# Layer 1 attention: softmax sums of two row blocks inverted in one instruction, the split of the probabilities two steps behind, attention output and projection one step later

## The chip, the cores and the metric

The kernel runs on one core of one Trainium2 chip, in one launch, and holds a whole two-layer model. The metric is the device time of one execution in microseconds. The engines that matter here are TensorE (PE in the profile; its weight loads are PEld), VectorE (DVE), ScalarE (ACT), GpSimd (POOL) and SyncE (SP), which issues most of the DMAs.

## The reference, cut to what matters

The input is `x` with 2 batches of 1024 rows of 512 numbers. Layer 0 is an attention with one head of 128 and a branch with a Sinkhorn iteration. Layer 1, which takes most of the time, is a causal attention with 32 query heads of 128, whose keys and values come in 8 groups (four query heads share one), and beside it a feed-forward part with a low-rank mixture of experts.

```python
xn = _layernorm(x)
x = x + _L1_attn_ref(xn, ...) + _L1_ffn_ref(xn, ...)

def _L1_attn_ref(hidden_states, Wq, Wk_down, Wv_down, Wk_up, Wv_up, Wo):
    q = ...                                       # 32 heads of 128
    k, v = ...                                    # 8 groups of 128, repeated 4 times
    scores = jnp.einsum('bhqd,bhkd->bhqk', q, k) * scale
    scores = jnp.where(causal, scores, -1e9)
    attn = jax.nn.softmax(scores, axis=-1)
    out = jnp.einsum('bhqk,bhkd->bhqd', attn, v)
    return out.transpose(0, 2, 1, 3).reshape(b, s, H * D) @ Wo.T
```

The change touches only how the softmax of layer 1 is divided by its sums, and when.

## The kernel before, in words

Every product of two float32 matrices is done with float16 pairs: each operand is kept as a high part and a low part (what the high part leaves over), and three matmuls (high by high, high by low, low by high) make one product. `mm3` (line 89) issues them for projections and scores, `attn_out` (line 365) for the product of probabilities and values.

Layer 1 runs over 16 groups `g`: eight key/value groups of batch 0 and then eight of batch 1. A group has 32 steps `s`. One step handles one row block: 32 query positions of four heads, which fill the 128 partitions, against the first W = 32(s+1) keys. What one row block goes through:

- scores on PE (`rows_scores`, line 89) into one PSUM bank of tag `s` up to W = 512, else into two; there are four such banks (`BS`)
- row maximum on DVE (`rows_exp`, lines 284 and 288), which also writes the scaled scores from PSUM into the SBUF tile `P`
- exponential on ACT (line 292), in place in `P`, which also adds up the row into the small tile `r`
- `rows_hi`: reciprocal of the sum on DVE (line 316), a scaling of it by 16384 on ACT (line 317), and the high part of the probabilities on ACT (line 322) into the tile `Phl`
- `rows_lo`: the low part on DVE (line 330; two instructions for some widths), a memset of padding on POOL (line 334), and a transposing DMA from `Phl` to the tile `PT` on SP's queue (line 335)

`row_step` interleaves two row blocks: in step s it emits the scores of block s, then `rows_hi` of block s-1, then the row maximum and exponential of block s, then `rows_lo` of block s-1. A list called `pending` holds the one block in between. `P` and `Phl` have three buffers each (`PB`, `LB`). A buffer of `P` holds four blocks for s below 8, two for s below 16, and one from there on. So from s = 16 the row maximum of block s+3 can only write once the low part of block s has been computed.

After each `row_step` come the other pieces of work that a table `fill` assigns to the step: query projections, keys and values of the next group, fetching and splitting weights (POOL, held behind the latest `rows_lo` by `behind`), and the work of the other parts of the model (`extra`). For each of the 16 pairs of row blocks the product with the values runs at step 4c + 2k + `AVD` (`av`; c counts blocks of four steps, k the pair in it), and for each c the output projection at step 4c + `WOD` (`wo`). A pair's `av` comes three steps after the step that emits the second transpose of the pair.

This text order is not the order on the engines. When the program is built, the framework's scheduler goes through a simulated time and gives each engine, whenever it is free, the earliest-written instruction that is ready. The order on each engine is then fixed, and on the chip each engine works through its list in order and waits at the head of it for the semaphores of the instruction there.

Layer 0 uses the same `row_step` with blocks of 128 rows.

Of the kernel before, what the change touches and what calls it, by code (L numbers as in the profile page):

```python
# [11 lines left out]
AF = mybir.ActivationFunctionType  # L12
# [4 lines left out]
P = 128  # L17
# [12 lines left out]
QR = 32  # L30
# [9 lines left out]
SK0, SKN, MX0, MXN, LN1 = 1, 116, 122, 74, 198  # L40

G0, G1, GL, WT, LX, LA = 16, 200, 3, 220, 231, 240
AVD, WOD = 5, 10
KVN, QN, QNN, QH = 19, 18, 24, 1
MG = range(8, 16)
FW, FF = 210, 221
# [2 lines left out]
PSCALE = 16384.0  # L49
# [3 lines left out]
def tile_model(ctx: ExitStack, tc: tile.TileContext, out: bass.AP, a: dict):  # L53
# [3 lines left out]
    V, A, G = nc.vector, nc.scalar, nc.gpsimd  # L57
# [7 lines left out]
    def T(tag, shape, dt=F32, bufs=None):  # L65
        count[0] += 1
        kw = {} if bufs is None else {"bufs": bufs}
        return sb.tile(shape, dt, tag=tag, name=f"{tag}_{count[0]}", **kw)
# [115 lines left out]
    last_hi, last_lo, last_low = [None], [None], [None]  # L184
# [87 lines left out]

    P_of, hl_of = [None], [None]

    def rows_exp(pieces, causal, scale, n, k):

        W = pieces[-1][0] + pieces[-1][1]
        Pm = share(P_of, n, k, lambda: T("P", [P, n, S // n], bufs=PB))
        nm = T("nm", [P, 2], bufs=4)
        last = None  # L280
        for k, (o, w, pt) in enumerate(pieces):
            first = 1.0e30 if last is None else last
            if causal and o + w == W:
                last_row[0] = V.tensor_tensor_reduce(Pm[:, o:o + w], pt[:, :w], mask[:, 512 - w:],  # L284
                                       -scale, first, ALU.add, ALU.min,
                                       nm[:, k:k + 1])
            else:
                last_row[0] = V.tensor_scalar(Pm[:, o:o + w], pt[:, :w], -scale, first,  # L288
                                ALU.mult, ALU.min, accum_out=nm[:, k:k + 1])
            last = nm[:, k:k + 1]  # L290
        r = T("r", [P, 2], bufs=4)
        A.activation(Pm[:, :W], Pm[:, :W], AF.Exp, bias=last, scale=-1.0,  # L292
                     accum_out=r[:, 0:1])
        return Pm, r, W

    def rows_parts(W, n, k, mix=False):

# [14 lines left out]
        v = hl.rearrange("p (l k) -> p l k", l=2)  # L312
        return hl, v[:, 0, :W], [(0, W, v[:, 1, :W])], v[:, :, W:] if W < m * P else None

    def rows_hi(Pm, r, W, pool, hl):
        V.reciprocal(r[:, 1:2], r[:, 0:1])  # L316
        A.activation(r[:, 1:2], r[:, 1:2], AF.Copy, scale=PSCALE)  # L317
        if pool:
            A.activation(Pm[:, :W], Pm[:, :W], AF.Copy, scale=r[:, 1:2])
            A.activation(hl[1], Pm[:, :W], AF.Copy)  # L320
        else:
            A.activation(hl[1], Pm[:, :W], AF.Copy, scale=r[:, 1:2])  # L322

    def rows_lo(Pm, r, W, pool, hl, dst):
        whole, hi, los, pad = hl
        for a0, a1, lo in los:
            if pool:
                G.tensor_tensor(lo, Pm[:, a0:a1], hi[:, a0:a1], ALU.subtract)
            else:
                last_low[0] = V.scalar_tensor_tensor(lo, Pm[:, a0:a1], r[:, 1:2], hi[:, a0:a1],  # L330
                                                     ALU.mult, ALU.subtract)
        if pad is not None:

            behind(G.memset(pad, 0.0), last_low[0])  # L334
        nc.sync.dma_start_transpose(dst[:, :whole.shape[1] // P], whole)  # L335

    pending = []

    def row_step(q=None, K=None, W=None, causal=None, scale=None, dst=None, pool=None, n=1, k=0,
                 mix=False):  # L340

        if q is not None:
            pieces = rows_scores(q, K, W)
        old = None
        if pending:
            old = pending.pop()
            rows_hi(*old[:5])
        if q is not None:
            pending.append((*rows_exp(pieces, causal, scale, n, k), pool, rows_parts(W, n, k, mix), dst))
        if old:  # L350
            rows_lo(*old)

    def out_tile():
        count[0] += 1
# [311 lines left out]
    SC1 = 1.0 / (math.sqrt(128.0) * 128.0)  # L666
# [108 lines left out]
    def fetch_q(g, hh):  # L775
        qw[g, hh] = fetch(a["Wq"][4 * (g % NG) + hh])
# [8 lines left out]
    def layer1_attn(kv0, start, extra):  # L785


        N, NS = NB * NG, S // QR
        fill = {}

        def at(g, s, f):
            g, s = g + s // NS, s % NS
            fill.setdefault((g, s), []).append(f)

        kvs, Qs, PTs, avs, aos, wos = [{} for _ in range(6)]

        def twice(g):
            Vm = kvs[g]["Vm"] = [T("xr", [P, NT, P], F16, bufs=XB) for l in range(2)]
            for l in range(2):
                for k in range(2):  # L800
                    nc.sync.dma_start(Vm[l][64 * k:64 * k + 64], kvs[g]["V"][0:64, l])

        def q_unit(g, u):
            half, hh = divmod(u, 4)
            if hh == 0:
                Qs[g, half] = T("Q", [P, 2, NS // 2, 4, QR], F16, bufs=2)
            qproj(g // NG, qw[g, hh], Qs[g, half], hh, half)

        def fetch_wo(g, hh):
            n = 4 * (g % NG) + hh  # L810
            wos[g, hh] = fetch(a["WoT"][n * P:(n + 1) * P, :])

        def split_wo(g, hh):
            wos[g, hh] = parts_of(wos[g, hh], "wo", 32.0, WB)

        def av(g, c, k):
            if k == 0:
                avs[g, c] = out_tile()
            aos[g, c] = group_av(kvs[g]["V"], kvs[g].get("Vm"), PTs[g, 2 * c + k], c, k, avs[g, c])

        def wo(g, c):
            wo_block(g // NG, c, aos[g, c], [wos[g, h] for h in range(4)], g % NG == NG - 1)

        kvs[0], fs = kv0
        start(fs[2:], lambda u: q_unit(0, u))
        for hh in range(4):
            fetch_wo(0, hh)
            split_wo(0, hh)
        for g in range(N):
            if g + 1 < N:  # L830
                new = (g + 1) % NG == 0
                kvs[g + 1], fs = kv((g + 1) // NG, (g + 1) % NG)
                at(g, KVN - 2 if new else 1, fs[0])
                for k, f in enumerate(fs[1:]):
                    at(g, KVN + 2 * k if new else 1 + 4 * k + 2 * (k == 0), f)
                for hh in range(4):
                    at(g, 5 + 4 * hh, lambda g=g, hh=hh: fetch_q(g + 1, hh))
                    at(g, 7 + 4 * hh, lambda g=g, hh=hh: split_q(g + 1, hh))
                for u in range(4):
                    at(g, QNN + 2 * u if new else QN + 4 * u, lambda g=g, u=u: q_unit(g + 1, u))  # L840
                for hh in range(4):
                    s = 26 + 2 * hh if new else 22 + 3 * hh
                    at(g, s - 2, lambda g=g, hh=hh: fetch_wo(g + 1, hh))
                    at(g, s, lambda g=g, hh=hh: split_wo(g + 1, hh))
            for u in range(4):
                at(g, QH + (1 if (g + 1) % NG == 0 else 3) * u, lambda g=g, u=u: q_unit(g, 4 + u))
            if g in MG:
                at(g, 2, lambda g=g: twice(g))
            for c in range(NT):
                for k in range(2):  # L850
                    at(g, 4 * c + 2 * k + AVD, lambda g=g, c=c, k=k: av(g, c, k))
                at(g, 4 * c + WOD, lambda g=g, c=c: wo(g, c))
        for k, fs in extra.items():
            fill[k] = fs + fill.get(k, [])
        for g in range(N + 1):
            for s in range(NS):
                if g < N:
                    c, r = divmod(s, NR)

                    n = 4 if c < 2 else 2 if c < 4 else 1  # L860
                    if c < 4 and r == 0:
                        PT = T("PT", [P, 2 * (c + 1), NR, P], F16, bufs=3)
                        for k in range(2):
                            PTs[g, 2 * c + k] = PT[:, :, 2 * k:2 * k + 2]
                    elif c >= 4 and r % 2 == 0:
                        PTs[g, s // 2] = T("PT", [P, 2 * (c + 1), 2, P], F16, bufs=3)
                    Qt, q0 = Qs[g, s // (NS // 2)], s % (NS // 2)
                    row_step(lambda l: Qt[:, l, q0].rearrange("p h q -> p (h q)"),
                             kvs[g]["K"], QR * (s + 1), True, SC1, PTs[g, s // 2][:, :, r % 2], False, n, r, g in MG)
                elif pending:  # L870
                    row_step()
                for f in fill.pop((g, s), []):
                    f()
        assert not fill, sorted(fill)
# [131 lines left out]
    PTs = attn0_rows(0, 0, *f0[0][:2], lambda: adv(CA))  # L1006
    ys0 = branch0(0, *f0[0][3:5], lambda: adv(CB))
    attn0_out(0, 0, f0[0][2], PTs)
    PTs = attn0_rows(0, 1, *f0[0][:2], lambda: adv(CA))
# [6 lines left out]
    for half in range(2):  # L1016
# [5 lines left out]
        PTs = attn0_rows(1, half, *f0[1][:2], lambda: adv(CD))  # L1022
# [153 lines left out]
```

## Time and profile before

| what | value |
|---|---|
| three runs | 1846.09, 1852.34, 1855.1 us; median 1852.34 us |
| profiled execution, span of the instructions | 1846.2 us (no separate time outside the span is listed) |
| PE busy | 1708.2 us, 93% |
| DVE busy | 1473.1 us, 80% |
| ACT busy | 1191.1 us, 65% |
| POOL busy | 896.5 us, 49% |
| layer 1's first scores | 263.7 us after the start |
| a group of batch 1 | 90 to 92 us for 32 steps |

The page of the profile has numbered parts: the busy time of each engine, the span in 40 slices, the DMA queues, the chain of work that ended last, and the costliest groups of instructions. A group's line gives the source line, engine, operation, tile written and tiles read, shapes and count, then the busy time and the mean of one in ns, then the idle time of the engine just before these instructions and what ended it. Busy times of matmuls are modelled, because matmuls overlap. The fastest run, 1846.09 us, is as long as the profiled span; the median of the runs is 6.1 us above the span.

### The profile page before, as it was taken

The page shows a single profiled execution, that of the slowest core. Times are in us where ns is not written, and L with a number is a line of the kernel's source. Part 1 is how long each engine was busy: PE and PEld are TensorE (multiplying, and loading weights), DVE is VectorE, ACT ScalarE, POOL GpSimd, SP SyncE. Part 2 cuts the span into 40 slices and gives each one's busy share as a digit, 9 for nine tenths or more (in the row PEclk, how much of TensorE's full clock was granted, in tenths as well). Part 3 has the DMA queues.
Part 4 walks back from the last instruction along what each step waited for, and adds up shares of the span by engine and source line. Part 5 has one row for each costly group of instructions (what it writes and reads, how often), then busy time and mean ns, then how long its engine had stood idle before and what let it go on. Part 6 is the DMA issues. An engine that isn't in the chain of part 4 may idle for free.

```text
span 1846.2 us, 35059 instructions
## 1 busy us (share of the span) xinstructions
PE 1708.2 (93%) x11394; PEld 1038.5 (56%) x11394; DVE 1473.1 (80%) x4162; ACT 1191.1 (65%) x2917; POOL 896.5 (49%) x1476
## 2 busy tenths in 40 slices
PE   4666389999999999998999999999999999999998
PEld 2434146566666566655555566666666666666565
DVE  8888968988888878778976768778787877787675
ACT  4848666656676778876544656667666767676564
POOL 5568629778766465647634433323242424235200
PEclk9888699999999999999999999999999999999999
DMA  7435225656575656468645656556566655566455
GB/s 212 82 56 132 59 44 123 151 118 139 119 149 98 141 128 144 105 142 143 146 98 125 144 126 140 135 124 141 125 134 124 142 118 142 124 143 135 97 121 118
DMA packets 693482, 230.25 MB, mean 125 GB/s; under 512 B 674081, under 2 KB 674209, under 8 KB 693298
## 3 DMA queue, kind: packets, MB, share of 16 engines
q1 hardware_dynamic: 677842, 180.75, 47.3%
q0 software_dynamic: 13152, 43.07, 8.7%
q10 hardware_dynamic: 2304, 4.20, 0.7%
q8 instruction: 89, 1.46, 0.3%
q14 instruction: 95, 0.78, 0.1%
HBM read 52.81 MB, written 4.19 MB: 31 GB/s over the span
## 4 chain that ended last, share of the span: by engine, by line
PE 47%; DVE 2%; DMA 1%; POOL 1%; issue 1%; ACT 0%; SPq 0%; DVEq 0%
PE pp L89 26%; PE av L365 11%; PE s L89 10%; DVE Phl L330 0%; DVE f2k L913 0%; DMA f2k<-in_Wq 0%; DMA xT<-wo 0%; DVE P L288 0%; POOL wo L241 0%; DMA PT<-Phl 0%; POOL f2k L95 0%; SPq L335 0%; DVE P L284 0%; DMA twT<-twhl 0%; DVE Q L106 0%
## 5 line engine op out<-in xcount | busy, mean ns | idle before, releaser
L292 ACT ACTIVATE P<-P,nm 128x1024 f32<-128x1024 f32 (+31 forms) x528 | 391.5, 742 | 280.9 <-DVE nm L284 263.4
L330 DVE SCALAR_TENSOR_TENSOR Phl<-P,r,Phl 128x64 f16<-128x64 f32 (+16 forms) x627 | 460.8, 759 | 75.7 <-ACT Phl L322 70.3
L89 PE MATMUL s<-K,Q 128*128 128x512 f16 (+22 forms) x2400 | 439.1, 317 | 19.7 <-DVE P L288 11.7
L365 PE MATMUL av<-PT,V 128*128 128x256 f16 x3456 | 425.6, 274 | 9.4 <-DMA PT<-Phl 8.5
L365 PEld LDWEIGHTS <-V 128*128 128x128 f16 x3456 | 338.2, 98 | 92.9 <-DMA PT<-Phl 10.6
L322 ACT ACTIVATE Phl<-P,r 128x1024 f16<-128x1024 f32 (+31 forms) x515 | 369.5, 730 | 20.6 <-DMA PT<-Phl 5.3
L89 PE MATMUL pp<-xT,wq 128*128 128x512 f16 x1536 | 371.8, 381 | 4.5 <-DVE Q L106 2.3
L89 PE MATMUL pp<-wo,ao 128*128 128x512 f16 x1536 | 369.9, 379 | 2.0 <-ACT ao L105 1.9
L95 POOL TENSOR_SCALAR f2k<-f2k 128x512 f32<-128x512 f32 x164 | 113.9, 695 | 500.6 <-DVE Phl L330 458.9
L89 PEld LDWEIGHTS <-Q 128*128 128x128 f16 x2400 | 222.8, 98 | 175.7 <-issue 27.7
L89 PEld LDWEIGHTS <-wq 128*128 128x128 f16 x1536 | 149.7, 98 | 172.6 <-issue 6.8
L89 PEld LDWEIGHTS <-ao 128*128 128x128 f16 x1536 | 149.5, 98 | 156.9 <-ACT ao L105 3.4
L284 DVE CUSTOM_DVE_ANT_0 P<-s,mask,nm 128x272 f32<-128x272 f32 (+15 forms) x256 | 157.3, 615 | 9.3 <-PE s L89 1.0
L288 DVE TENSOR_SCALAR_CACHE_REDUCE P<-s 128x512 f32<-128x512 f32 (+15 forms) x272 | 152.6, 562 | 13.4 <-PE s L89 11.2
L316 DVE RECIPROCAL r<-r 128x1 f32<-128x1 f32 x528 | 78.9, 154 | 87.5 <-ACT P L292 84.5
L317 ACT ACTIVATE r<-r 128x1 f32<-128x1 f32 x528 | 95.6, 192 | 60.2 <-DVE r L316 59.7
L105 ACT ACTIVATE ao<-av 128x512 f16<-128x512 f32 x128 | 74.9, 585 | 81.7 <-PE av L365 81.5
L334 POOL MEMSET Phl<- 128x192 f16 (+1 forms) x320 | 56.2, 189 | 142.3 <-DMA PT<-Phl 97.3
L105 ACT ACTIVATE Q<-pp 128x512 f16<-128x512 f32 x128 | 74.6, 583 | 64.3 <-PE pp L89 60.0
L284 DVE CUSTOM_DVE_ANT_0 P<-s,mask 128x32 f32<-128x32 f32 (+15 forms) x256 | 103.7, 430 | 14.9 <-PE s L89 14.2
L755 DVE SCALAR_TENSOR_TENSOR acc<-pp,acc 128x512 f32<-128x512 f32 x128 | 87.1, 681 | 35.1 <-PE pp L89 34.7
L106 DVE SCALAR_TENSOR_TENSOR Q<-pp,Q 128x512 f16<-128x512 f32 x128 | 87.4, 683 | 34.0 <-ACT Q L105 33.7
(256 smaller groups left out, 2153.1 us busy)
## 6 DMA issues: line engine op xcount, KB each, us to landing
f2k<-in_Wq POOLq DMA_DIRECT2D x64, 256.0 KB, 3.1
f2k<-in_WoT POOLq DMA_DIRECT2D x64, 256.0 KB, 3.3
PT<-Phl SPq DMA_TRANSPOSE x528, 3.2
acc<-in_x SPq DMA_DIRECT2D x16, 256.0 KB, 5.1
f2k<-in_Wup POOLq DMA_DIRECT2D x16, 256.0 KB, 3.3
out<-acc ACTq DMA_DIRECT2D x16, 256.0 KB, 3.5
xr<-V SPq DMA_DIRECT2D x32, 128.0 KB, 2.4
xr<-in_x SPq DMA_DIRECT2D x12, 256.0 KB, 3.9
```

Source lines behind the costliest of these rows:

```text
L89: nc.tensor.matmul(dst, lhs(l), rhs(r), start=(i == 0 and j == 0), stop=(i == n - 1 and j == 2))
L95: first = G.tensor_scalar(stage, stage, scale, 1.0, ALU.mult, ALU.mult)
L105: A.activation(hl_hi, src, AF.Copy, scale=scale)
L106: return V.scalar_tensor_tensor(hl_lo, src, scale, hl_hi, ALU.mult, ALU.subtract)
L284: last_row[0] = V.tensor_tensor_reduce(Pm[:, o:o + w], pt[:, :w], mask[:, 512 - w:], -scale, first, ALU.add, ALU.min, nm[:, k:k + 1])
L288: last_row[0] = V.tensor_scalar(Pm[:, o:o + w], pt[:, :w], -scale, first, ALU.mult, ALU.min, accum_out=nm[:, k:k + 1])
L292: A.activation(Pm[:, :W], Pm[:, :W], AF.Exp, bias=last, scale=-1.0, accum_out=r[:, 0:1])
L317: A.activation(r[:, 1:2], r[:, 1:2], AF.Copy, scale=PSCALE)
L322: A.activation(hl[1], Pm[:, :W], AF.Copy, scale=r[:, 1:2])
L330: last_low[0] = V.scalar_tensor_tensor(lo, Pm[:, a0:a1], r[:, 1:2], hi[:, a0:a1], ALU.mult, ALU.subtract)
L365: nc.tensor.matmul(p, v, pt, start=(k == 0), stop=(k == len(todo) - 1))
L755: V.scalar_tensor_tensor(acc[b, t], p, 1.0 / 256.0, acc[b, t], ALU.mult, ALU.add)
```

## The change

In layer 1 two consecutive row blocks share one tile `r` of four columns: two sums and two inverses. One reciprocal and one scaling handle both columns; this happens when the first of the two blocks gets its high part. The list `pending` now holds two blocks, so that step s emits `rows_hi` and `rows_lo` of block s-2 instead of s-1. On an even step the reciprocal needs the exponentials of blocks s-2 and s-1; on an odd step nothing new is inverted. After the last step of the last group the two blocks that are left are handled together. `AVD` and `WOD` are each larger by one, so `av` and `wo` move one step later in the text. Layer 0 keeps one block per tile `r` and one step of distance (`rows=1`).

```diff
-AVD, WOD = 5, 10
+AVD, WOD = 6, 11
...
-    def rows_exp(pieces, causal, scale, n, k):
+    def rows_exp(pieces, causal, scale, n, k, total):
...
-        r = T("r", [P, 2], bufs=4)
         A.activation(Pm[:, :W], Pm[:, :W], AF.Exp, bias=last, scale=-1.0,
-                     accum_out=r[:, 0:1])
-        return Pm, r, W
+                     accum_out=total)
+        return Pm, W
...
-    def rows_hi(Pm, r, W, pool, hl):
-        V.reciprocal(r[:, 1:2], r[:, 0:1])
-        A.activation(r[:, 1:2], r[:, 1:2], AF.Copy, scale=PSCALE)
+    def rows_inverse(r):
+        n = r.shape[1] // 2
+        V.reciprocal(r[:, n:], r[:, :n])
+        A.activation(r[:, n:], r[:, n:], AF.Copy, scale=PSCALE)
+
+    def rows_hi(Pm, W, inv, pool, hl):
         if pool:
-            A.activation(Pm[:, :W], Pm[:, :W], AF.Copy, scale=r[:, 1:2])
+            A.activation(Pm[:, :W], Pm[:, :W], AF.Copy, scale=inv)
             A.activation(hl[1], Pm[:, :W], AF.Copy)
         else:
-            A.activation(hl[1], Pm[:, :W], AF.Copy, scale=r[:, 1:2])
+            A.activation(hl[1], Pm[:, :W], AF.Copy, scale=inv)
...
-    pending = []
+    pending, sums, left = [], [None], [0]
...
         if q is not None:
             pieces = rows_scores(q, K, W)
-        old = None
-        if pending:
-            old = pending.pop()
-            rows_hi(*old[:5])
+        old = []
+        if pending and (q is None or len(pending) == pending[0][2]):
+            old = [pending.pop(0)] if q is not None else pending[:]
+            if q is None:
+                pending.clear()
+            for o in old:
+                if o[3]:
+                    rows_inverse(o[1])
+                rows_hi(*o[0][:5])
         if q is not None:
-            pending.append((*rows_exp(pieces, causal, scale, n, k), pool, rows_parts(W, n, k, mix), dst))
-        if old:
-            rows_lo(*old)
+            if left[0] == 0:
+                sums[0], left[0] = T("r", [P, 2 * rows], bufs=4), rows
+            r, i = sums[0], rows - left[0]
+            left[0] -= 1
+            Pm, w = rows_exp(pieces, causal, scale, n, k, r[:, i:i + 1])
+            pending.append(((Pm, w, r[:, rows + i:rows + i + 1], pool, rows_parts(W, n, k, mix), dst),
+                            r, rows, i == 0))
+        for o in old:
+            rows_lo(*o[0])
```

In `layer1_attn` the call of `row_step` gets one more argument, `rows` = 2.

More of the change, by code (lines that the diff above doesn't have):

```diff
@@ L313, in rows_parts, with rows_lo @@
         return hl, v[:, 0, :W], [(0, W, v[:, 1, :W])], v[:, :, W:] if W < m * P else None
-    def rows_hi(Pm, r, W, pool, hl):
-        V.reciprocal(r[:, 1:2], r[:, 0:1])
-        A.activation(r[:, 1:2], r[:, 1:2], AF.Copy, scale=PSCALE)
+    def rows_inverse(r):
[3 more added lines that the diff above has]
+    def rows_hi(Pm, W, inv, pool, hl):
         if pool:
-            A.activation(Pm[:, :W], Pm[:, :W], AF.Copy, scale=r[:, 1:2])
+            A.activation(Pm[:, :W], Pm[:, :W], AF.Copy, scale=inv)
             A.activation(hl[1], Pm[:, :W], AF.Copy)
         else:
-            A.activation(hl[1], Pm[:, :W], AF.Copy, scale=r[:, 1:2])
-    def rows_lo(Pm, r, W, pool, hl, dst):
+            A.activation(hl[1], Pm[:, :W], AF.Copy, scale=inv)
+    def rows_lo(Pm, W, inv, pool, hl, dst):
         whole, hi, los, pad = hl
@@ L329, in rows_lo @@
             else:
-                last_low[0] = V.scalar_tensor_tensor(lo, Pm[:, a0:a1], r[:, 1:2], hi[:, a0:a1],
+                last_low[0] = V.scalar_tensor_tensor(lo, Pm[:, a0:a1], inv, hi[:, a0:a1],
                                                      ALU.mult, ALU.subtract)
@@ L335, in rows_lo @@
         nc.sync.dma_start_transpose(dst[:, :whole.shape[1] // P], whole)
-    pending = []
+    pending, sums, left = [], [None], [0]
     def row_step(q=None, K=None, W=None, causal=None, scale=None, dst=None, pool=None, n=1, k=0,
-                 mix=False):
+                 mix=False, rows=1):
         if q is not None:
             pieces = rows_scores(q, K, W)
-        old = None
-        if pending:
-            old = pending.pop()
-            rows_hi(*old[:5])
-        if q is not None:
-            pending.append((*rows_exp(pieces, causal, scale, n, k), pool, rows_parts(W, n, k, mix), dst))
-        if old:
-            rows_lo(*old)
+        old = []
[7 more added lines that the diff above has]
+                rows_hi(*o[0][:5])
+        if q is not None:
+            if left[0] == 0:
[7 more added lines that the diff above has]
+            rows_lo(*o[0])
     def out_tile():
@@ L868, in layer1_attn @@
                     row_step(lambda l: Qt[:, l, q0].rearrange("p h q -> p (h q)"),
-                             kvs[g]["K"], QR * (s + 1), True, SC1, PTs[g, s // 2][:, :, r % 2], False, n, r, g in MG)
+                             kvs[g]["K"], QR * (s + 1), True, SC1, PTs[g, s // 2][:, :, r % 2], False, n, r, g in MG, 2)
                 elif pending:
```

## The prediction

> **What bounds the kernel now.** I read the page first: the shares of the engines, the 40 slices, the chain, and the two groups that the change halves.
>
> ```profile
> PE 1708.2 (93%) x11394; PEld 1038.5 (56%) x11394; DVE 1473.1 (80%) x4162; ACT 1191.1 (65%) x2917; POOL 896.5 (49%) x1476
> PE   4666389999999999998999999999999999999998
> PE 47%; DVE 2%; DMA 1%; POOL 1%; issue 1%; ACT 0%; SPq 0%; DVEq 0%
> L316 DVE RECIPROCAL r<-r 128x1 f32<-128x1 f32 x528 | 78.9, 154 | 87.5 <-ACT P L292 84.5
> L317 ACT ACTIVATE r<-r 128x1 f32<-128x1 f32 x528 | 95.6, 192 | 60.2 <-DVE r L316 59.7
> ```
>
> PE is the bound from slice 6 on, and the chain runs through it. The idle time before L316 and L317 (84.5 and 59.7 us) is no sum to collect: it is idle time of DVE and ACT, neither of them the bound.
>
> Next come PE's own waits from 255 us to the end (layer 1; releaser, us in total, times, longest), since only these can be won.
>
> ```profile
> PE s L89 <- DVE nm L284: 6.7, 7, 1.6
> PE av L365 <- DMA PT<-Phl: 4.0, 3, 2.2
> PE s L89 <- DVE P L288: 3.7, 3, 1.7
> PE pp L89 <- DVE Q L106: 2.3, 2, 1.9
> PE pp L89 <- DVE acc L755: 2.2, 1, 2.2
> ```
>
> The rest of that answer adds up to 8.8 us, none of it from a row block. The first and third lines are PE waiting for a bank of `s`, that is for DVE to take a row maximum. Seven of the ten waits lie within the first six blocks of a group, after the widest rows of the group before: 1.0, 0.9 and 1.3 us at 357 to 360, 1.0 at 455, 0.7 at 548, 0.8 at 641, 1.6 at 831; the others are 0.2 at 265, 1.1 at 749 and 1.7 at 919. Between 1050 and 1700 us the same question gives no line at all.
>
> The busy times by stretch show what that means, and what a wait costs beyond its length (columns: PE, PEld, DVE, ACT, POOL busy with counts; granted clock; DMA share; GB/s).
>
> ```profile
> 355.00:361.00 6.00, 2.83 (x25) 1.81 (x24) 5.87 (x19) 4.21 (x10) 4.37 (x11) 0.90 0.90 203
> 361.00:366.00 5.00, 5.00 (x24) 2.47 (x23) 5.00 (x22) 3.69 (x15) 3.75 (x9) 0.77 0.68 161
> 844.00:848.00 4.00, 4.00 (x23) 2.96 (x22) 3.81 (x16) 3.01 (x11) 2.89 (x4) 0.57 0.60 122
> 861.20:865.50 4.30, 4.28 (x13) 1.61 (x13) 3.16 (x7) 1.61 (x4) 1.38 (x3) 0.60 1.04 225
> 1100.00:1740.00 640.00, 640.00 (x4256) 395.59 (x4255) 506.45 (x1422) 428.01 (x1040) 228.74 (x382) 1.00 0.61 131
> ```
>
> In 640 us of batch 1 PE is never idle, at full clock, with DVE at 79% and ACT at 67%: no change in DVE or ACT can shorten that stretch. After a wait of 2.2 us PE runs at 0.57 for 4 us, so lost clock adds to the price.
>
> [...]
>
> **The change, part by part** (sum against the profiled execution, 1846.2 us).
>
> 1. *Half of the reciprocals and scalings go.* Layer 1 has 16 × 32 = 512 row blocks, so 256 of each. A reciprocal costs 78.9/528 = 0.149 us, a scaling 95.6/528 = 0.181 us: 38 us of DVE and 46 us of ACT. The new ones have two columns: the nearest row is the one-column one; the 32-column reciprocal of the Sinkhorn chain (0.35 us) bounds it above. On PE's path all this is 0 in batch 1.
>
> 2. *PE waits in batch 0.* The ceiling is the five lines, 18.9 us, and the lost clock after them: 5 × 0.23 + 4 × 0.43 + 4.3 × 0.40 = 4.6 us; together 23.5 us. The `s` lines are DVE backlog of about 1 us each (10.4 us in ten waits). In the last eight steps of a group the change takes four reciprocals off DVE (0.6 us). Between 255 and 1050 us DVE also stands at the head of its list before L316 49 times for 30.9 us, some 1.5 times in such eight steps; half of that goes: 0.75 × 0.63 = 0.5 us. So 1.1 us against waits of 1 us, but the scheduler writes a new order, and I take two thirds of 10.4 + 1.2 us: −8. The other lines concern a transpose, a query projection and a late accumulation at the batch change, where nothing is removed in particular: 0. Where a bank wait goes, PE has its next matmuls ready: what is late next is the same kind of wait at the next group's start, already counted. Bounds: 0 and −23.5 us.
>
> 3. *Two blocks pending in three buffers of `P`.* From s = 16 the row maximum of block n+3 needs the low part of block n. For even n that low part now follows the exponential of n+1. Group 11, n = 22 (W = 736, next 768; the last line is the maximum of block 25):
>
> ```profile
> 1421.72 1.09 DVE L330 SCALAR_TENSOR_TENSOR Phl<-P,r,Phl 128x736 f16<-128x736 f32 x1
> 1423.38 0.94 ACT L292 ACTIVATE P<-P,nm 128x768 f32<-128x768 f32 x1 [0.52 <-DVE nm L284]
> 1426.19 0.57 DVE L288 TENSOR_SCALAR_CACHE_REDUCE P<-s 128x416 f32<-128x416 f32 x1
> ```
>
> The exponential and its sum end at 1424.40. Reciprocal, scaling, high part (0.91) and low part (1.09) with their hand-overs make 2.7 us: 1427.1, 0.9 us after block 25's maximum began. That maximum would end at 1430.3, and PE takes the scores of block 27, which need its banks, only at 1432.69: hidden with 2.4 us to spare. The same arithmetic over all 16 groups finds 34 such places, at rows 16 to 28, in all 40 us late; PE's spare time is less than the lateness at four of them (groups 2, 3, 4 and 8), by 1.3, 1.0, 0.5 and 0.7 us: +3.5 us. Bounds: 0, if the scheduler fills PE otherwise, and +40, if no spare time is left.
>
> [...]
>
> 4. *The wait that is added.* The reciprocal of an even step waits, as before, for the exponential just before it; behind it on DVE stand the next row maximum and `rows_lo`. On odd steps there is no such wait. Transposes come one step later, and so do `av` and `wo`: the distance from the second transpose of a pair to its `av` stays three steps, on SP's queue and for `PT`'s three buffers. POOL's weight splits wait for the latest low part, which is one block older in the text but computed at the same step: 0. `wo` of one group now frees its weight buffers one step later, in group 7 in the very step in which the first normalised tile of batch 1 asks for the ninth of nine: +0.5 (0 to +3, the nearest row being 1.2 us of PE waiting for xT).
>
> 5. *The tail.* Blocks 30 and 31 are inverted together after the last exponential.
>
> ```profile
> 1825.79 1.13 ACT L292 ACTIVATE P<-P,nm 128x1024 f32<-128x1024 f32 x1
> 1828.74 1.29 DVE L330 SCALAR_TENSOR_TENSOR Phl<-P,r,Phl 128x1024 f16<-128x1024 f32 x1 [0.53 <-ACT Phl L322]
> 1835.85 2.78 PE L365 MATMUL av<-PT,V 128*128 128x256 f16 x24
> ```
>
> The last low part ends at 1830.0; with 3.2 us for the transpose (DMA issues, median) it lands at 1833.2, and PE takes it at 1835.85. With the high and low part of block 30 ahead of it, it is 1.3 us later: 1834.5, still hidden. I take +0.5 (0 to +2).
>
> Sum: −8 + 3.5 + 0.5 + 0.5 = −3.5, so 1842.7 us for an execution like the profiled one. The median of the runs lies 6.1 us above that one: **1848.8 us**, say 1849.
>
> **The rivals.** *DVE is freed more than I grant* (faster). For it: DVE's shorter list also ends its waits before L330 (26.4 us from 255 to 1050), and its lateness is what the acc and Q lines show. Against it: half of PE's waits here have other causes. Between two thirds of the 23.5 us and all of it, with the +1 of parts 4 and 5: 1838 to 1830 us. *The buffers of `P` become the bound* (slower): where DVE and ACT are behind, as in batch 0 (low part of group 3's row 26: 3.3 us late), block n+3 waits, PE's spare time is used up, and later rows inherit it. It decides once lateness exceeds, as a rule, the 2 to 6 us of spare time that most places have. Half of the 40 us and no gain: 1852.3 + 20 + 1 = 1873; a quarter: 1863. Against it: batch 1 has the spare time in every group. *The pairing doesn't do what it says*: the reciprocals that remain are just those that wait for a fresh exponential, so DVE's idle time stays, and no PE wait goes: 1852.3 + 4.5 = 1857 us.
>
> **How the numbers follow.** A measurement of this kernel can tell about 0.5% from no change: 1843.1 to 1861.6 us. My forecast has 0.36, the pairing without effect 0.14, both within that; the faster rival 0.27; the slower one 0.23. The predicted time is the forecast's. The range 1830 to 1870 us reaches to all of the faster rival and to most of the slower one, and leaves out about 2 in 10.
>
> **What would show it.** L316 and L317 should count 272 each. PE should stay without waits from 1100 to 1740 us, and the `s` lines should fall from 10.4 us to about 3. I am wrong if PE waits for L284 or L288 in the late rows of each group (buffers of `P`), if the granted clock dips in batch 1, or if the batch change near 840 to 940 us loses much more or less than now.

## The result and the profile after

The changed kernel takes 1875.24 us (median of four runs, 1872.87 to 1877.04), the kernel before 1852.86 us in the same comparison: a ratio of 1.0129, interval 1.0108 to 1.0151. It is slower by 1.3%, some 22 to 24 us, outside the range given. The profiled execution has a span of 1875.2 us inside a time of 1877.04 us, so 1.8 us lie around the span.

The lines of the page that answer to those shown of before:

```profile
PE 1714.1 (91%) x11394; PEld 1039.7 (55%) x11394; DVE 1441.8 (77%) x3906; ACT 1159.1 (62%) x2661; POOL 895.1 (48%) x1476
PE   4756389999999999899998999999999999999998
PE 37%; issue 2%; DVE 2%; ACT 2%; DVEq 0%; ACTq 0%
PE pp L89 20%; PE av L378 9%; PE s L89 8%; ACT Phl L324 1%; ACT P L291 1%; DVE Phl L332 1%; DVE P L284 0%; DVE P L288 0%; DVE cmp L106 0%; DVE ao L106 0%; DVE acc L768 0%; ACT Q L105 0%; ACT r L317 0%; ACT ao L105 0%; DVE nm L284 0%
L316 DVE RECIPROCAL r<-r 128x2 f32<-128x2 f32 (+1 forms) x272 | 43.2, 159 | 87.2 <-ACT P L291 84.5
```

The work was saved as planned: 256 fewer reciprocals, DVE 31 us less busy, ACT 32 us less. But the idle time that ends at the exponential (L291 now) is the same 84.5 us before about half as many reciprocals (272 instead of 528). The chain's ACT share went from 0% to 2%: the exponential (L291) and the high part (L324) now stand in the chain with 1% each.

PE's own waits from 255 us to the end, the first six lines:

```profile
PE s L89 <- DVE nm L284: 11.5, 14, 2.3
PE pp L89 <- DMA xT<-wo: 7.3, 1, 7.3
PE pp L89 <- ACT ao L105: 7.2, 8, 1.3
PE pp L89 <- DMA wo<-xr: 4.4, 3, 2.1
PE s L89 <- DVE P L288: 4.1, 3, 1.8
PE av L378 <- DMA PT<-Phl: 4.1, 5, 2.1
```

The waits for a bank of `s` grew from 10.4 to 15.6 us. Over 640 us of batch 1, where PE had no wait at all, it is now idle for 4.7 us (same columns as in the prediction's table):

```profile
1110.00:1750.00 640.00, 635.27 (x4208) 391.46 (x4205) 481.29 (x1291) 410.85 (x917) 234.42 (x379) 1.00 0.61 130
```

Lost clock explains little of it: from 255 us on, the last 4 us left out, PE's granted clock is 0.5 for 17.1 us in this trace and for 13.7 us in the one before.

From the first scores of one group to those of the next, the 29.0 us by which the two profiled spans differ (the medians differ by 22.4) lie here:

| stretch | before | after | difference |
|---|---|---|---|
| up to the first scores of layer 1 | 263.7 | 265.8 | +2.1 |
| groups 0 to 2 | 283.0 | 284.5 | +1.5 |
| groups 3 to 5 | 279.1 | 296.2 | +17.1 |
| groups 6 and 7 (batch change) | 260.4 | 262.3 | +1.9 |
| groups 8 to 14 | 636.7 | 642.9 | +6.2 |
| group 15 and the end | 123.3 | 123.5 | +0.2 |

The loss is worst in groups 3 to 5. There ACT was busiest before: 71%, 77% and 80% of the group, against 65% to 66% in groups 0 to 2 and 67% in batch 1. That this is why is not shown. In group 4 the loss can be read line by line. A selection of DVE's and ACT's lines in order of time, blocks 28 (W = 928) to 31 (W = 1024):

```profile
736.51 0.65 DVE L288 TENSOR_SCALAR_CACHE_REDUCE P<-s 128x480 f32<-128x480 f32 x1
739.17 1.10 ACT L291 ACTIVATE P<-P,nm 128x960 f32<-128x960 f32 x1 [3.86 <-DVE nm L284]
740.39 0.17 DVE L316 RECIPROCAL r<-r 128x2 f32<-128x2 f32 x1 [0.57 <-ACT P L291]
741.64 2.05 ACT L324 ACTIVATE Phl<-P,r 128x928 f16<-128x928 f32 x2
742.74 2.32 DVE L332 SCALAR_TENSOR_TENSOR Phl<-P,r,Phl 128x928 f16<-128x928 f32 x2 [1.60 <-ACT Phl L324]
744.97 0.69 DVE L288 TENSOR_SCALAR_CACHE_REDUCE P<-s 128x512 f32<-128x512 f32 x1
```

This is a closed loop. The maximum of block 29 begins at 736.51; its exponential runs to 740.3; only then comes the reciprocal of the pair 28 and 29, then the high and low parts of both. The maximum of block 31, which needs the buffer of `P` that 28 gives up, stands behind them on DVE and begins at 744.97. The loop takes 8.46 us for two blocks. DVE waits 0.57 and 1.60 us inside it, and ACT 3.86 us, most of it inside.

A turn of 8.46 us is not long by itself; what is new is that no turn is short. The row maxima of blocks 27, 29 and 31, first before (block 27 to 29 in 4.14 us, 29 to 31 in 9.29), then block 27 after (7.81 us to the next):

```profile
717.18 0.61 DVE L288 TENSOR_SCALAR_CACHE_REDUCE P<-s 128x448 f32<-128x448 f32 x1
721.32 0.63 DVE L288 TENSOR_SCALAR_CACHE_REDUCE P<-s 128x480 f32<-128x480 f32 x1
730.61 0.69 DVE L288 TENSOR_SCALAR_CACHE_REDUCE P<-s 128x512 f32<-128x512 f32 x1
```

```profile
728.70 0.61 DVE L288 TENSOR_SCALAR_CACHE_REDUCE P<-s 128x448 f32<-128x448 f32 x1
```

From the maximum of block 17 to that of block 31 in group 4, two blocks took 4.1 to 9.4 us before and 51.8 us went by in all; after, every two blocks take 7.1 to 9.1 us, 57.2 us in all. DVE can no longer catch up. PE meets the lateness in the next group:

```profile
745.72 0.29 PE L89 MATMUL s<-K,Q 128*128 128x96 f16 x3 [1.82 <-DVE P L288]
758.49 1.76 PE L89 MATMUL s<-K,Q 128*128 128x288 f16 x10 [2.31 <-DVE nm L284]
```

### The profile page after: what moved, and what is told of

Same layout as the page of the kernel before. It is cut to its first block, busy times and chain, and to the rows that moved or that the text cites. A ratio compares the mean times of both kernels' runs of the same rounds, so it can differ in the third digit from the quotient of the medians.

```text
span 1875.2 us, 34674 instructions
## 1 busy us (share of the span) xinstructions
PE 1714.1 (91%) x11394; PEld 1039.7 (55%) x11394; DVE 1441.8 (77%) x3906; ACT 1159.1 (62%) x2661; POOL 895.1 (48%) x1476
## 5 line engine op out<-in xcount | busy, mean ns | idle before, releaser
L291 ACT ACTIVATE P<-P,nm 128x1024 f32<-128x1024 f32 (+31 forms) x528 | 391.4, 742 | 327.0 <-DVE nm L284 318.3
L332 DVE SCALAR_TENSOR_TENSOR Phl<-P,r,Phl 128x64 f16<-128x64 f32 (+16 forms) x627 | 447.7, 751 | 116.5 <-ACT Phl L324 113.1
L89 PE MATMUL s<-K,Q 128*128 128x512 f16 (+22 forms) x2400 | 444.0, 317 | 24.6 <-DVE P L288 11.6
L89 PE MATMUL pp<-xT,wq 128*128 128x512 f16 x1536 | 366.6, 379 | 2.2 <-DVE acc L768 0.7
L95 POOL TENSOR_SCALAR f2k<-f2k 128x512 f32<-128x512 f32 x164 | 121.7, 743 | 513.9 <-DVE Phl L332 455.1
L324 ACT ACTIVATE Phl<-P,r 128x1024 f16<-128x1024 f32 (+31 forms) x515 | 349.9, 728 | 15.8 <-DMA PT<-Phl 6.5
L284 DVE CUSTOM_DVE_ANT_0 P<-s,mask,nm 128x272 f32<-128x272 f32 (+15 forms) x256 | 157.1, 618 | 13.5 <-PE s L89 2.7
L288 DVE TENSOR_SCALAR_CACHE_REDUCE P<-s 128x512 f32<-128x512 f32 (+15 forms) x272 | 151.9, 562 | 18.6 <-PE s L89 16.6
L284 DVE CUSTOM_DVE_ANT_0 P<-s,mask 128x32 f32<-128x32 f32 (+15 forms) x256 | 106.0, 430 | 21.8 <-PE s L89 21.4
L316 DVE RECIPROCAL r<-r 128x2 f32<-128x2 f32 (+1 forms) x272 | 43.2, 159 | 87.2 <-ACT P L291 84.5
L106 DVE SCALAR_TENSOR_TENSOR ao<-av,ao 128x512 f16<-128x512 f32 x128 | 87.4, 683 | 29.5 <-ACT ao L105 29.4
```

The costliest lines, as they stand in the source:

```text
L89: nc.tensor.matmul(dst, lhs(l), rhs(r), start=(i == 0 and j == 0), stop=(i == n - 1 and j == 2))
L95: first = G.tensor_scalar(stage, stage, scale, 1.0, ALU.mult, ALU.mult)
L106: return V.scalar_tensor_tensor(hl_lo, src, scale, hl_hi, ALU.mult, ALU.subtract)
L324: A.activation(hl[1], Pm[:, :W], AF.Copy, scale=inv)
L332: last_low[0] = V.scalar_tensor_tensor(lo, Pm[:, a0:a1], inv, hi[:, a0:a1], ALU.mult, ALU.subtract)
```

## The experiments

Two numbers from the traces are used throughout. *Holding time* is the time from the start of a block's row maximum to the end of its low part, as a mean over the even blocks from s = 16 on in groups 9 to 14: how long such a block keeps a buffer of `P`. *Overhang* is the time from the first scores of the next group to the end of the last low part of this one, in the same groups: how far the row blocks are behind PE. Before, they were 7.0 and 4.8 us; after, 9.6 and 6.1 us. For odd blocks the holding time is 7.0 us in both. Each ratio is to runs of the kernel before on the same chip.

**A fourth buffer of `P`, and `av` and `wo` put back or moved alone.** Theory A held the buffers responsible, theory B the later `av` and `wo`, theory C the mere fact of a new order of instructions.

```diff
-FB, PB, LB, XB, WB = 4, 3, 3, 4, 9
+FB, PB, LB, XB, WB = 4, 4, 3, 4, 9
...
-            y = T("ysum", [P, P], bufs=8) if b else ya[:, t % 4]
+            y = T("ysum", [P, P], F16, bufs=8) if b else ya[:, t % 4]
```

The last two lines and four tiles that move into other tiles' buffers (not shown) make the room; the next run does the same to the kernel before.

> The changed kernel with a fourth buffer of P (room made by keeping ysum in float16, half its bytes, and by putting four small tiles of the feed-forward part and of the weights into buffers that are idle by then). Theory A, buffers of P (two blocks pending in three buffers, so the low part of an even block gates the row maximum three blocks on): the time goes back to 1845 to 1858 us, DVE's wait at L332 for L324 falls from 113 us to under 90, and the 0.9 us stall per group of batch 1 goes. Theory B, the later av and wo: no change, 1870 to 1880 us. Theory C, any rewritten order of instructions costs some 20 us by chance: 1860 to 1890 us, with the stalls at other places.

Measured: 1862.03 us, ratio 1.0063 (1.0045 to 1.0080). Half of the loss is gone, short of what theory A expected, but with its signs: DVE's wait at L332 (low part) for L324 (high part) fell to 87.7 us, the overhang to 4.3 us, and PE has no wait between 1180 and 1740 us. The holding time stays at 9.8 us: the fourth buffer doesn't shorten the even block's hold, it lets one block more begin meanwhile. The short turns are back: in group 4 the maxima of blocks 17 to 31 take 48.6 us instead of 57.2. What is left of the loss lies in groups 3 to 5, which take 290.9 us against 279.2 in the kernel before with four buffers.

> The kernel before with the same fourth buffer of P and the same room made. Theory A: it had one buffer to spare already, so 1845 to 1858 us. Theory B: the same, 1845 to 1858 us. Theory C: a new order, 1860 to 1890 us.

Measured: 1855.14 us, 1.0009 (0.9994 to 1.0025). The kernel before has no use for a fourth buffer. Theory C is not borne out: this rewritten program doesn't cost 20 us, nor do five below (1.0036 at most).

```diff
-AVD, WOD = 6, 11
+AVD, WOD = 5, 10
```

> The changed kernel with av and wo at their old steps (5 and 10). Theory A: no gain, 1868 to 1885 us, and av waits longer for its transposes. Theory B: most of it comes back, 1850 to 1860 us. Theory C: 1860 to 1890 us.

Measured: 1876.82 us, 1.0131 (1.0113 to 1.0148). Nothing comes back: theory B falls as the explanation of the whole.

```diff
-AVD, WOD = 5, 10
+AVD, WOD = 6, 11
```

> The kernel before with only av and wo one step later (6 and 11). Theory A: no loss, 1846 to 1860 us. Theory B: the whole loss, 1868 to 1880 us. Theory C: 1860 to 1890 us.

Measured: 1858.17 us, 1.0040 (1.0025 to 1.0055), in the kernel before. So the later `av` and `wo` cost some 7 us there. The time is inside theory A's range, but theory A, which held that they cost nothing, has no account of the 7 us, and theory B expected far more (1868 us at least).

**The pairing undone, with the two steps kept.** Each block gets its own `r`; the parts stay two steps behind.

```diff
...
             for o in old:
-                if o[3]:
-                    rows_inverse(o[1])
+                rows_inverse(o[1])
                 rows_hi(*o[0][:5])
...
+            r = T("r", [P, 2], bufs=4)
```

> The changed kernel with the pairing undone: each block keeps its own sum, reciprocal and scaling, done just before its high part, so L316 counts 528 again; two steps behind, three buffers of P, av and wo at 6 and 11 as in the change. Theory D, two blocks pending in three buffers is enough by itself: 1868 to 1882 us, with the 0.9 us stall per group of batch 1. Theory E, the pairing makes the buffers scarce because the even block's inverse waits for the odd block's exponential: 1855 to 1866 us, no stall in batch 1.

Measured: 1856.07 us, 1.0036 (1.0022 to 1.0050). Holding time 7.1 us, overhang 4.7 us, with the same three buffers. Theory E holds, theory D doesn't: two blocks pending in three buffers are no burden as long as neither waits for the other. Though the parts are written two steps behind, the block keeps its buffer no longer than before (7.1 against 7.0 us). DVE's waits, first after the change, then here:

```profile
DVE Phl L332 <- ACT Phl L324: 113.1, 127, 2.3
DVE r L316 <- ACT P L291: 84.5, 105, 4.3
```

```profile
DVE Phl L332 <- ACT Phl L324: 91.2, 156, 4.4
DVE r L316 <- ACT P L291: 54.3, 105, 2.9
```

With the pairing, DVE waits 30 us longer before half as many reciprocals, and 22 us longer before the low parts.

```diff
+        if pending:
+            rows_inverse(pending[-1][1])
...
```

> As the run with the pairing undone, but each block's reciprocal and scaling come one step behind as before the change, and only the high and low parts and the transpose two steps behind. Theory D: 1868 to 1882 us, as the buffers of P are held as long. Theory E: 1852 to 1864 us, and DVE's wait at L332 for L324 below 90 us.

Measured: 1853.59 us, 1.0018 (1.0005 to 1.0030). Holding time 7.1 us, and DVE's wait at L332 is 86.9 us, as theory E expected.

The fourth buffer together with the old steps of `av` and `wo`, in the changed kernel:

> The changed kernel with the fourth buffer of P and with av and wo back at 5 and 10. If the 10 us that stay with the fourth buffer are those of av and wo one step later (6 us were measured for that alone in the kernel before): 1851 to 1858 us. If they belong to the two steps of distance: 1860 to 1870 us.

Measured: 1864.66 us, 1.0084 (1.0061 to 1.0108). Neither of the changed kernel's forms gets `av`'s 7 us back by the old steps; what stays with the fourth buffer is not that. The time lies in the range given for the two steps of distance, but the two kernels without the pairing have that distance too and lose 0.36% and 0.18%, so the distance by itself does not explain it either.

The kernel before with two buffers of `P`:

> The kernel before with two buffers of P: one block pending and one being written, so as little to spare as the change leaves with three. Theory A, no buffer of P to spare is what costs: slower than before by 10 to 40 us, 1862 to 1892 us, with stalls in batch 1 at least as long per group as after the change (groups of 91.8 us or more, against 90.9). Otherwise: 1846 to 1858 us.

Measured: 1876.84 us, 1.0146 (1.0128 to 1.0165), inside theory A's range and yet without its sign. Of the 33.4 us by which this profiled span is longer than that of before, 17.5 us arise before layer 1's first scores (281.2 us against 263.7), where layer 0's blocks fill a buffer each, and 8.0 us in groups 0 to 2. Groups 10 to 14 take 90.9 us each and PE loses nothing in them. A block holds its buffer there for 6.2 us, which is 3.1 us for each of two buffers; after the change it is 8.3 us as a mean over even and odd blocks, only 2.8 us for each of three, and PE does lose. So neither the number of spare buffers nor the holding time per buffer decides alone. What this kernel doesn't have is a hold that hangs on the next block's exponential.

**The wait alone, the common tile alone.** The first of these kernels has all 528 reciprocals and adds only the wait, the second has the common tile without it.

```diff
+        i = V.reciprocal(r[:, n:], r[:, :n])
+        if wait is not None:
+            behind(i, wait, True)
...
+                mate = last_exp[0] if o[2] > 1 and o[3] else None
+                rows_inverse(o[1], mate)
...
+            r = T("r", [P, 2], bufs=8)
```

> Own sum, reciprocal and scaling for each block as in the run with the pairing undone (528 reciprocals), and one wait added: the reciprocal of an even block waits for the exponential of the odd block after it, as the pairing makes it. Theory E, it is that wait that costs: 1868 to 1882 us, even blocks from W = 544 on hold P some 9 to 10 us against 7, the stall in batch 1 is back. Theory F, the common tile r or the fewer instructions lie behind it: 1852 to 1862 us.

Measured: 1881.19 us, 1.0154 (1.0131 to 1.0177). Holding time 9.6 us, overhang 6.0 us. PE's waits from 1180 to 1740 us, first in the changed kernel, then with the pairing undone, then with the wait added:

```profile
PE s L89 <- DVE nm L284: 3.5, 5, 0.7
PE pp L89 <- ACT ao L105: 1.2, 1, 1.2
```

```profile
PE av L373 <- DVE ao L106: 0.2, 1, 0.2
PE s L89 <- DVE P L288: 0.2, 1, 0.2
```

```profile
PE s L89 <- DVE nm L284: 4.0, 5, 0.8
PE pp L89 <- ACT ao L105: 0.2, 1, 0.2
```

The added wait brings back the five stalls and the whole loss (1.0154 against the change's 1.0129, with overlapping intervals). Beside the wait, this kernel differs from the one with the pairing undone only in eight buffers instead of four for the small tile `r`.

```diff
-                if o[3]:
-                    rows_inverse(o[1])
...
+        if pending:
+            rows_inverse(pending[-1][1], pending[-1][0][2])
```

> Two blocks share the tile r of four columns as in the change, but each column is inverted and scaled by itself, one step behind, so the even block waits for nothing of the odd one. Theory E: 1850 to 1860 us, as with own tiles. Theory F, the common tile: 1868 to 1882 us.

Measured: 1856.09 us, 1.0030 (1.0021 to 1.0040). The common tile is harmless.

> Own inverses one step behind, high and low parts two steps behind in the text, av and wo at their old steps 5 and 10: the two-step distance by itself. If the distance costs nothing and the later av and wo are what remains: 1846 to 1855 us. If the distance costs: 1856 to 1866 us.

Measured: 1855.02 us, 1.0017 (1.0004 to 1.0029). The time touches the upper end of the first range: writing the parts a step later costs about 3 us, some 5 us at most by the interval. Here the old `av` and `wo` make no difference to the run with the early inverses (1.0018), so the 7 us of moving them were seen in the kernel before only.

```diff
-            old = [pending.pop(0)] if q is not None else pending[:]
-            if q is None:
-                pending.clear()
+            old = pending[:]
+            pending.clear()
```

> Pairs inverted together as in the change, but on each even step the parts of both blocks are emitted (two steps and one step behind), none on odd steps, av and wo at 5 and 10. Theory E: the even block still holds P until the odd one's exponential is done, so 1865 to 1885 us. If the second block's later place is what costs: 1850 to 1862 us.

Measured: 1873.19 us, 1.0119 (1.0096 to 1.0142). The even block still waits for the odd one (holding time 10.4 us), and the loss is there.

**Which blocks.** Pairs for one half of a group's blocks, own inverses one step behind for the other.

```diff
...
+        if pending and pending[-1][3]:
+            rows_inverse(pending[-1][1])
...
+                             kvs[g]["K"], QR * (s + 1), True, SC1, PTs[g, s // 2][:, :, r % 2], False, n, r, g in MG, 2, s < 16)
```

This is the narrow half; the wide one has `s >= 16` in the last line.

> Pairs are inverted together only for the first 16 blocks of a group (W up to 512, where a buffer of P holds two or four blocks); the blocks from W = 544 on keep their own inverse, one step behind. Two steps behind and av and wo at 6 and 11 throughout. If the wait costs only where a buffer of P holds one block: as with own inverses, 1848 to 1857 us, half of the instructions saved and perhaps 1 to 3 us of it seen. If it costs through the length of the chain anywhere: 1860 to 1870 us.

Measured: 1850.91 us, 0.9998 (0.9985 to 1.0011). Pairing the narrow blocks costs nothing. Against own inverses throughout (1.0018) it is 0.2% better, about 4 us, though the two intervals overlap.

> The other half: pairs only for the blocks from W = 544 on, own inverses before. If the wait costs only where a buffer of P holds one block: nearly the whole loss, 1868 to 1880 us. If it costs anywhere: 1860 to 1870 us.

Measured: 1870.77 us, 1.0111 (1.0090 to 1.0133). Nearly the whole loss, with a holding time of 9.6 us and an overhang of 6.2 us. The wait costs in the wide half, where a buffer of `P` holds one block, and nothing in the narrow half, whose inverses wait in the same way. That fits the buffers, but the wide blocks also have the longest exponentials and parts (in the trace after an exponential takes 1.15 us at a width of 1024 and 0.71 at 512, the high part 1.14 and 0.71, the low part 1.33 and 0.90), and this pair of runs does not separate the two. That the buffers carry a share is shown by the fourth one, which takes back half of the loss.

## Why the prediction was wrong, step by step

*What bounds the kernel* was right: PE, with nothing to win in batch 1.

*Part 1* was right: 256 instructions each went, at 159 and 195 ns for two columns against 154 and 192 for one; the two groups' busy time fell by 35.7 and 43.4 us (38 and 46 predicted). *Part 5* was right in kind: the low part of the last block ends 5.8 us after its exponential began, against 4.2 before, and the last `av` still waits for PE, not for it.

*Part 2* failed. The gain of 8 us supposed that half of DVE's waits before L316 go with half of the instructions. Nothing went where it was supposed to: between 255 and 1050 us these waits are 50 with 42.8 us, against 49 with 30.9 us before, and over the whole run 143 waits became 105 longer ones with the same total of 84.5 us. The `s` waits grew instead of falling to 3 us. The prediction had said itself, in its third rival, that the reciprocals that remain are just those that wait for a fresh exponential. (Its sum of PE's other waits, 8.8 us, should be 8.4; nothing rests on it.) What the saved instructions are worth by themselves shows in two pairs of runs: 1.0154 with the wait and all instructions against 1.0129 with the wait and half of them, and 1.0018 against 0.9998 without it in the wide half, where the narrow half's instructions go. Both point to about 4 us, but the intervals overlap in each pair, so this is not shown.

*Part 3* is the step that decided, and it was mis-sized. It found the right mechanism, the places (rows 16 to 28) and a first lateness of about 1 us, and then compared each lateness with PE's spare time *of the kernel before*, place by place: +3.5 us. But block n+3, late by 1 us, is itself the odd block that the next pair's inverse waits for. The lateness goes round the loop: in group 4 no two blocks go faster than 7.1 us, where before they could take 4.1. In group 5 PE pays for it: the time between matmul starts, beyond the median that a matmul of that width takes in these traces, adds up to about 14 us, against 1.4 before. PE's waits for L284 and L288 came not in the late rows of a group, where the prediction looked for them, but in the first rows of the next. The wait costs 1.0154 against 1.0036, that is 0.0118 of 1852 us or 22 us (some 17 to 27 by the two intervals), about half of the 40 us that the prediction gave as its upper bound. The slower rival named this, its loop ("later rows inherit it") and nearly its time (1873 us against 1875.24). That its time came so close is partly luck: half of the 40 us was a choice, not a sum, and the stated range ended short of it. Its chance of 0.23 was too small: what spoke against it was the spare time of batch 1, and most of the loss (17.1 of 29.0 us) lies in groups 3 to 5 of batch 0.

The prediction expected PE without waits from 1100 to 1740 us. The trace after has a wait of 0.7 us there at the same block (W = 224) of five groups in a row, 3.5 us in all; with the fourth buffer PE has no wait between 1180 and 1740 us. The spare time of before, on which the expectation rested, did not hold.

*Part 4* priced the later `av` and `wo` at 0.5 us. Alone, in the kernel before, they cost 0.40% or 7 us; in the changed kernels, moving them back brings nothing. Why they cost that in the kernel before stays open: in its trace groups 0 and 3 are 4 and 5 us longer, and PE's waits for L288 are 7.4 us against 3.7. What remains of the loss with a fourth buffer (0.63%, in groups 3 to 5) is also not settled: the added wait alone brings the whole loss, but only half of it is shown to come by way of the buffers of `P`.

## What to carry to other kernels

Combining small instructions of two blocks ties the first block to the second, and the price is not the instruction but what the first block holds while it waits: here a buffer of `P` for 9.6 instead of 7.0 us. Where such a hold closes a loop (the freed buffer admits the block that the next release waits for), compare the length of the whole loop with the time the bound engine takes for the blocks in it, over many blocks (57.2 against 51.8 us here), and not each lateness with the spare time measured before the change. Combine where blocks are short and a buffer holds several of them, as the narrow half did for free.

## What the runs showed of the hardware

Whether PE's clock fell behind a wait did not follow from the wait's length alone. In the trace after, the granted clock is 0.50 for 3.41 us (839.39 to 842.80 and 880.35 to 883.76 us) behind single waits of 2.1 us that end at 839 and 879 us, and stays at 1.00 behind waits of 2.3 us to 758, 2.0 to 902 and 2.0 to 948. Stretches of 3.41 us around three of these waits, two by two (PE's busy time is the first number behind the length, the granted clock the third from the end):

```profile
754.06:757.47 3.41, 2.12 (x16) 1.36 (x14) 2.49 (x3) 3.14 (x7) 0.00 (x0) 1.00 0.00 0
757.47:760.88 3.41, 2.03 (x12) 1.16 (x12) 3.41 (x13) 2.02 (x8) 2.54 (x3) 1.00 1.20 261
835.98:839.39 3.41, 1.32 (x8) 0.57 (x7) 3.41 (x8) 0.38 (x1) 3.11 (x3) 1.00 1.24 148
839.39:842.80 3.41, 3.41 (x18) 2.44 (x17) 1.00 (x5) 3.20 (x7) 2.30 (x5) 0.50 0.92 200
945.20:948.61 3.41, 1.48 (x7) 0.60 (x7) 3.41 (x13) 1.87 (x3) 3.30 (x5) 1.00 0.78 163
948.61:952.02 3.41, 3.19 (x35) 2.83 (x35) 3.27 (x15) 2.60 (x6) 0.98 (x3) 1.00 0.00 0
```

In the 3.41 us before 839.39 PE is idle for 2.09 us, and in the 3.41 us behind them it has half the clock. The wait to 758 is longer, but the two stretches in which it lies have 1.29 and 1.38 us of idle time, and the clock stays at 1.00; so it does behind the stretch with 1.93 us of idle time before 948.61. What decides, beyond the length, these few waits do not show.
